# Joined count banks, shared sum and block banks, degrees through DRAM and fewer signals in a two-layer graph network kernel

## The chip, the cores and the metric

The kernel runs on one core of a Trainium2 chip. The metric is device time in microseconds; a lower number is better. Several runs are timed and one more is profiled. Engines are named as the profile names them: PE (matrix products), PEld (its weight loads), DVE (vector), ACT (scalar), POOL (GpSimd, which here issues the indirect gathers) and SP (which here issues most other DMAs).

## What is computed

A graph with 12,500 nodes of 256 features and 200,000 edges, sorted by their destination, goes through two layers that average over neighbours, a last product, and a residual with layer norm:

```python
def _sage_conv(x, src, dst, W_l, b_l, W_r):
    msgs = x[src]
    agg = jax.ops.segment_sum(msgs, dst, num_segments=N_NODES)
    deg = jax.ops.segment_sum(jnp.ones((src.shape[0],), x.dtype), dst, num_segments=N_NODES)
    mean = agg / jnp.maximum(deg, 1.0)[:, None]
    return mean @ W_l + b_l + x @ W_r
h = jax.nn.relu(_sage_conv(x, src, dst, W1_l, b1, W1_r))
h = jax.nn.relu(_sage_conv(h, src, dst, W2_l, b2, W2_r))
x = _layernorm(x + h @ W3 + b3, axis=-1)
```

Destinations are drawn as a squared uniform number, so low-numbered nodes have many edges and high-numbered ones few.

## The kernel before, in words

The edges lie in tiles of 128 (`NT` = 1563), the nodes in 98 blocks of 128. Two ways of summing neighbours run side by side in each layer.

**Gathered destinations.** Destinations beyond the first 1280 (layer 1) or 1792 (layer 2) are summed from gathered rows. A round (`Gathers.gathered`, L237) takes four edge tiles: POOL issues four indirect DMAs (L243), each fetching 128 rows of 256 floats into one of four `got` buffers. PE then multiplies each tile by a 0/1 selection of 32 columns (`one`, made by DVE at L201, two rounds ahead), so that four strips of 32 rows of one PSUM bank hold sums (L254; in layer 1 a 257th column of ones counts edges). A group has one or two rounds. At its end ACT copies the strips to SBUF (L259). `summed` (L262) multiplies them by a second selection `two` (L265) to place 128 sums, transposed, in PSUM; in layer 1 another product at L270 places the edge counts in one row. DVE adds both into a ring of 8 blocks (`degs` L273, `sums` L277). Layer 1 has 269 rounds and 186 groups, layer 2 has 247 rounds and 175 groups.

**Counted destinations.** The first destinations are done in seven groups of 256 with a matrix of edge counts. `count` (L646) builds it: for each edge tile DVE makes a selection of (destination, source block) pairs (`pick`, L661, three buffers, two tiles ahead) and of the source's low bits (L665); PE multiplies them (L706, L710 adds the edges that the next tile shares). A tile covers 5, 7 or 9 destinations of 98 source blocks each, 490, 686 or 882 columns. One PSUM bank holds 512, so 7 and 9 take two `halves`, each with a bank of `count_pool` (three banks) and a copy by ACT (L712, or an add by DVE at L697 for the first 128 tiles). `product` (L628) then multiplies the counts by all node rows, split into three bf16 parts: 98 steps of six matmuls (L638); SP loads `rows` for two steps at a time (L635, 384 KB, three buffers). `split_rows` (L622) makes the three parts of x for layer 1: SP loads a block, ACT and DVE take turns on it (L617 to L620), SP stores it (L626).

**Blocks.** When a block's sums are complete, `first_block` (L878, three pieces) or `last_block` (L902, five pieces) computes its output: load x or h, transpose it on PE (L839) and copy it on ACT (L842), multiply by both weights (`sage`, L863 and L865), add bias and scale by the reciprocal degree on DVE (L868, L869), apply relu on ACT (L871), store. For a ring block of layer 1, PE turns the row of degrees into a column with a matmul by one (L886), the same ACT copy brings it out, and DVE makes the reciprocal (L889, L890). ACT zeroes the used part of the ring (L894, L895, L913).

**Order.** PE and POOL keep the order in which the program is written (L421: `manual_schedule`); for DVE, ACT and SP a scheduler picks the order from estimated times, and each engine runs its own order strictly. `layer` (L562) writes the order: each round has three turns; in each, `pieces` advances one block piece (at most two blocks at a time, a block at most every second turn, `MOST, APART = 2, 2`), and `fill` adds steps of the counted work up to a cost that is due by then (`COST_DENSE`, `count_cost`). Stage 0 of layer 1 mixes counting with the 98 splits; later stages mix counting one group with the product of the one before.

**PSUM.** There are eight banks: one for strips (`part_ps`), one for `sum_ps`, two for blocks (`block_ps`), one for the product (`dense_ps`) and three for counts (`count_ps`):

```python
    sum_pool = ctx.enter_context(tc.tile_pool(name="sum_ps", bufs=1, space=PSUM))
    block_pool = ctx.enter_context(tc.tile_pool(name="block_ps", bufs=2, space=PSUM))
    dense_pool = ctx.enter_context(tc.tile_pool(name="dense_ps", bufs=1, space=PSUM))
    count_pool = ctx.enter_context(tc.tile_pool(name="count_ps", bufs=3, space=PSUM))
```

Of the kernel before, what the change touches and what calls it, by code (L numbers as in the profile page):

```python
# [7 lines left out]
F32 = mybir.dt.float32  # L8
# [11 lines left out]
POOL = mybir.EngineType.Pool  # L20

# [26 lines left out]
def by_runs(  # L48
# [80 lines left out]
    count_d = dram.tile([HG1 - 1, P, NB, DN], BF16, name="count_d")  # L129

# [43 lines left out]
    sum_pool = ctx.enter_context(tc.tile_pool(name="sum_ps", bufs=1, space=PSUM))  # L174
# [41 lines left out]
    class Gathers:  # L216
# [20 lines left out]
        def gathered(self, i):  # L237

            (gr, r), g = self.rounds[i], got[i % NGOT]
            t0, n = groups[gr]  # L240
            for j in range(G):
                e = t0 + j * n + r - C0 * P
                nc.gpsimd.indirect_dma_start(  # L243
                    out=g[:, j, :D], out_offset=None, in_=self.table,
                    in_offset=bass.IndirectOffsetOnAxis(ap=src_t[:, e:e + 1], axis=0))
            if i + AHEAD < len(self.rounds):
                self.chosen[i + AHEAD] = select(*self.rounds[i + AHEAD], self.second)
# [5 lines left out]
            for j in reversed(range(G)):  # L253
                nc.tensor.matmul(part_ps[j * W:(j + 1) * W, :width], lhsT=one[:, j],  # L254
                                 rhs=g[:, j, :width], start=r == 0, stop=r == n - 1)
# [6 lines left out]
        def summed(self, gr, some, two, done):  # L262
            sum_ps = sum_pool.tile([P, NC + 1, P], F32, name="sum_ps")
# [5 lines left out]
            if self.width > D:  # L269
                nc.tensor.matmul(sum_ps[0:1, NC], lhsT=some[:, D:D + 1], rhs=two,  # L270
# [284 lines left out]
    block_pool = ctx.enter_context(tc.tile_pool(name="block_ps", bufs=2, space=PSUM))  # L555
    dense_pool = ctx.enter_context(tc.tile_pool(name="dense_ps", bufs=1, space=PSUM))
    count_pool = ctx.enter_context(tc.tile_pool(name="count_ps", bufs=3, space=PSUM))
# [70 lines left out]
    def product(g, table3, c_sb):  # L628
# [3 lines left out]
        for b in range(NB):  # L632
            if b % 2 == 0:
                rows = work.tile([P, 2, 3, D], BF16, name="rows", bufs=3)
                nc.sync.dma_start(rows, table3[:, b:b + 2])  # L635
            for k in range(3):
                for c in range(NC):
                    nc.tensor.matmul(ps[:, c], lhsT=rows[:, b % 2, k, c * P:(c + 1) * P],  # L638
                                     rhs=c_sb[:, b, :DN],
                                     start=False, stop=b == NB - 1 and k == 2 and c == NC - 1)  # L640
            yield COST_DENSE
# [4 lines left out]
    def count(g, to):  # L646
# [32 lines left out]
        for t in range(lo_g, highs[g]):  # L679
# [5 lines left out]
            halves = [(0, w)] if w * NB <= 512 else [(0, w - w // 2), (w - w // 2, w)]  # L685
            if t < FIRST:
                j = t % G
                if j == 0:
                    pss = [count_pool.tile([P, 512], F32, name="count_ps") for _ in halves]
                for (a, b), ps in zip(halves, pss):  # L690
                    nc.tensor.matmul(ps[:, :(b - a) * NB], lhsT=s, rhs=r[:, a * NB:b * NB],
                                     start=j == 0, stop=j == G - 1)
                if j == G - 1:
                    n0 = off_dve.at(t - j)
                    for (a, b), ps in zip(halves, pss):
                        into = to[:, :, bass.ds(n0 + a, b - a)]
                        nc.vector.tensor_tensor(  # L697
                            into, into, ps[:, :(b - a) * NB].rearrange("p (d s) -> p s d", s=NB),
                            op=OP.add)
                yield count_cost(t)  # L700
            else:
                n0 = off_act.at(t)
                for a, b in halves:
                    ps = count_pool.tile([P, 512], F32, name="count_ps")
                    alone = a > 0 or before is None
                    nc.tensor.matmul(ps[:, :(b - a) * NB], lhsT=s, rhs=r[:, a * NB:b * NB],  # L706
                                     start=True, stop=alone)
                    if not alone:

                        nc.tensor.matmul(ps[:, :NB], lhsT=before[0], rhs=before[1],  # L710
                                         start=False, stop=True)
                    nc.scalar.copy(to[:, :, bass.ds(n0 + a, b - a)],  # L712
                                   ps[:, :(b - a) * NB].rearrange("p (d s) -> p s d", s=NB))
                    yield count_cost(t) / len(halves)
# [113 lines left out]
    def load_rows(table, n_rows, b, name):  # L828
        t = work.tile([P, D], F32, name=name)
# [6 lines left out]
    def transposed(t, ps, name, more=0):  # L836
# [481 lines left out]
```

## Time and profile before

| | |
|---|---|
| median of three runs | 2908.94 us (2904.64 to 2911.25) |
| profiled execution | 2910.6 us, span 2908.8 us |
| mean granted clock of PE | 0.914 |
| gathers of x (layer 1) | 1076, mean 1038 ns; the last ends at 1566 us |
| gathers of h (layer 2) | 988, mean 958 ns; from 1598 to 2856 us |
| products L638 | 7056, mean 279 ns, 976.9 us |
| count copies L712 on ACT | 1052 in three forms: 128x294 mean 650, 128x392 mean 663, 128x490 mean 721 ns |
| edge-count product L270 | 372 records (two to an fp32 matmul), 74.6 us |
| degree turn L886 | 176 records, 35.9 us |

In the profile an fp32 matmul shows as two records. Matmuls overlap, so the mean of a record is longer than the step from one start to the next. `L243 POOL ... x1076 | 1116.7, 1038 | 446.5 <-issue 274.2` reads: 1076 instructions, 1116.7 us busy, 1038 ns each, and the engine stood idle for 446.5 us before them, 274.2 of it with nothing in the profile to wait for.

### The profile page before, as it was taken

What the parts mean: (1) busy time and instruction counts of PE and PEld (TensorE: products, weight loads), DVE (VectorE), ACT (ScalarE), POOL (GpSimd) and SP (SyncE); (2) the same over time, 40 slices, a digit from 0 to 9 for tenths busy, and PEclk for the clock granted to TensorE, in tenths of its full rate; (3) what the DMA queues carried; (4) which work ended last, traced back from release to release, by engine and by line L of the source; (5) the groups of instructions that cost most, each with busy time, mean ns of one, the idle gap of its engine ahead of it and who ended that gap; (6) DMA issues with size and microseconds to landing.
All of it is one profiled execution on the core that took longest, in us unless ns stands there. A gap on an engine that the chain in (4) does not pass through costs nothing.

```text
span 2908.8 us, 54100 instructions
## 1 busy us (share of the span) xinstructions
PE 2394.6 (82%) x18630; PEld 1632.6 (56%) x18630; DVE 1471.2 (51%) x4350; ACT 1253.6 (43%) x2702; POOL 2065.3 (71%) x2074
## 2 busy tenths in 40 slices
PE   3475755898998999999996677877889898899995
PEld 1132323565665666666764455555666666677774
DVE  6687764664554565566564124434323333444443
ACT  0422764675675676677673014444112122222222
POOL 5777764777777777777774777777777777777772
PEclk9676767998999999999998899889999999999998
DMA  4455668877877878767864677777989989888872
GB/s 124 128 174 164 198 188 271 260 232 235 277 228 247 273 227 292 248 215 225 251 203 124 214 246 231 219 220 230 296 284 305 299 287 291 276 265 266 266 251 71
DMA packets 408133, 676.44 MB, mean 233 GB/s; under 512 B 59659, under 2 KB 266537, under 8 KB 407849
## 3 DMA queue, kind: packets, MB, share of 16 engines
q1 hardware_dynamic: 303415, 400.51, 42.5%
q0 software_dynamic: 99072, 270.66, 30.5%
q8 instruction: 149, 2.44, 0.3%
q10 hardware_dynamic: 5362, 1.72, 0.3%
q14 instruction: 135, 1.11, 0.1%
HBM read 582.80 MB, written 89.87 MB: 231 GB/s over the span
## 4 chain that ended last, share of the span: by engine, by line
PE 54%; DMA 19%; POOL 8%; issue 7%; DVE 6%; ACT 4%; DVEq 0%; SPq 0%; ACTq 0%; POOLq 0%
PE dense_ps L638 19%; POOL got L243 8%; PE part_ps L254 7%; PE block_ps L863 6%; DMA got<-h_d,src_t 5%; PE count_ps L706 5%; PE block_ps L865 5%; PE sum_ps L265 4%; DMA x_sb<-in_x_dram 3%; DMA rows<-h_d 3%; DMA rows<-x_d 3%; PE block_ps L839 2%; PE block_ps L921 2%; DMA split_sb<-in_x_dram 2%; PE sum_ps L270 2%
## 5 line engine op out<-in xcount | busy, mean ns | idle before, releaser
L243 POOL DMA_INDIRECT got<-in_x_dram,src_t x1076 | 1116.7, 1038 | 446.5 <-issue 274.2
L243 POOL DMA_INDIRECT got<-h_d,src_t x988 | 946.4, 958 | 343.1 <-issue 285.3
L638 PE MATMUL dense_ps<-counts,rows 128*128 128x256 bf16 x7056 | 976.9, 279 | 51.3 <-DMA rows<-h_d 27.7
L712 ACT CAST counts<-count_ps 128x392 f32 (+2 forms) x1052 | 717.6, 682 | 290.2 <-PE count_ps L710 174.0
L638 PEld LDWEIGHTS <-rows 128*128 128x128 bf16 x7056 | 671.3, 100 | 287.5 <-issue 88.6
L254 PE MATMUL part_ps<-got,one 128*32 128x257 f32 (+1 forms) x4128 | 359.7, 422 | 192.1 <-DMA got<-h_d,src_t 123.0
L706 PE MATMUL count_ps<-pick,low 128*128 128x392 bf16 (+2 forms) x1052 | 343.4, 354 | 57.0 <-ACT counts L712 27.0
L661 DVE TENSOR_SCALAR pick<-steps,key_t 128x686 bf16<-128x686 f16 (+2 forms) x748 | 301.4, 413 | 127.6 <-PE count_ps L706 110.2
L201 DVE TENSOR_TENSOR one<-lo_t,lane_b 128x128 f32<-128x128 bf16 x516 | 149.1, 289 | 372.7 <-PE part_ps L254 370.5
L259 ACT COPY some<-part_ps 128x257 f32<-128x257 f32 (+1 forms) x361 | 136.1, 377 | 431.4 <-PE part_ps L254 428.2
L254 PEld LDWEIGHTS part_ps<-got,one 128*32 128x32 f32 x4128 | 85.9, 111 | 323.5 <-issue 176.4
L265 PE MATMUL sum_ps<-two,some 128*128 128x128 f32 x1444 | 238.2, 290 | 0.2 <-DVE sums L277 0.2
L265 PEld LDWEIGHTS sum_ps<-two,some 128*128 128x128 f32 x1444 | 205.0, 201 | 20.5 <-issue 8.7
L277 DVE TENSOR_TENSOR sums<-sums,sum_ps 128x256 f32 x361 | 148.4, 411 | 132.6 <-PE sum_ps L265 101.9
L868 DVE TENSOR_TENSOR own<-block_ps,biases 128x256 f32<-128x256 f32 x196 | 83.0, 423 | 230.9 <-PE block_ps L865 230.2
L706 PEld LDWEIGHTS <-low 128*128 128x128 bf16 x1052 | 101.8, 100 | 152.3 <-DVE pick L661 54.2
L842 ACT COPY own_t<-block_ps 128x256 f32<-128x256 f32 (+1 forms) x294 | 110.0, 375 | 123.7 <-PE block_ps L839 121.2
L871 ACT ACTIVATE h<-own 128x256 f32<-128x256 f32 x196 | 81.4, 415 | 179.3 <-DVE own L869 179.2
L665 DVE TENSOR_TENSOR low<-low_t,lane_b 128x512 bf16<-128x512 bf16 x187 | 127.9, 684 | 21.1 <-PE count_ps L710 20.5
L710 PE MATMUL count_ps<-aft,low 128*128 128x98 bf16 x614 | 131.9, 215 | 0.0
L863 PE MATMUL block_ps<-w1l_sb,sums 128*128 128x256 f32 x352 | 113.9, 452 | 2.1 <-DVE sums L277 1.8
L863 PE MATMUL block_ps<-w2l_sb,sums 128*128 128x256 f32 x336 | 104.1, 437 | 11.3 <-DVE sums L277 11.1
(180 smaller groups left out, 2495.1 us busy)
## 6 DMA issues: line engine op xcount, KB each, us to landing
rows<-h_d SPq DMA_DIRECT2D x343, 384.0 KB
rows<-x_d SPq DMA_DIRECT2D x245, 384.0 KB
count_d<-counts SPq DMA_DIRECT2D x28, 896.0 KB
counts<-count_d SPq DMA_DIRECT2D x28, 896.0 KB
x_sb<-in_x_dram SPq DMA_DIRECT2D x194, 128.0 KB
x_d<-parts SPq DMA_DIRECT2D x98, 192.0 KB
h_d<-parts SPq DMA_DIRECT2D x98, 192.0 KB
got<-in_x_dram,src_t POOLq DMA_INDIRECT x1076
```

The costliest lines, as they stand in the source:

```text
L201: nc.vector.tensor_tensor(one, lo[:, a:a + n * (G - 1) + 1:n].unsqueeze(2).to_broadcast([P, G, W]), lane_b[:, :W].unsqueeze(1).to_broadcas ...
L243: nc.gpsimd.indirect_dma_start(out=g[:, j, :D], out_offset=None, in_=self.table, in_offset=bass.IndirectOffsetOnAxis(ap=src_t[:, e:e + 1], ...
L254: nc.tensor.matmul(part_ps[j * W:(j + 1) * W, :width], lhsT=one[:, j], rhs=g[:, j, :width], start=r == 0, stop=r == n - 1)
L259: nc.scalar.copy(some[:, :width], part_ps[:, :width])
L265: nc.tensor.matmul(sum_ps[:, c], lhsT=some[:, c * P:(c + 1) * P], rhs=two, start=True, stop=True)
L277: nc.vector.tensor_add(own, own, sum_ps[:, :NC])
L638: nc.tensor.matmul(ps[:, c], lhsT=rows[:, b % 2, k, c * P:(c + 1) * P], rhs=c_sb[:, b, :DN], start=False, stop=b == NB - 1 and k == 2 and ...
L661: nc.vector.tensor_scalar(r[:, :w * NB], steps[:, :w * NB], key_t[g][:, t - lo_g:t - lo_g + 1], None, op0=OP.is_equal)
L706: nc.tensor.matmul(ps[:, :(b - a) * NB], lhsT=s, rhs=r[:, a * NB:b * NB], start=True, stop=alone)
L712: nc.scalar.copy(to[:, :, bass.ds(n0 + a, b - a)], ps[:, :(b - a) * NB].rearrange("p (d s) -> p s d", s=NB))
L863: nc.tensor.matmul(ps[:, 0], lhsT=agg[:, c], rhs=wl[:, c], start=c == 0, stop=c == NC - 1)
L865: nc.tensor.matmul(ps[:, 1], lhsT=own_t[:, c], rhs=wr[:, c], start=c == 0, stop=c == NC - 1)
```

## The change

Six edits are made together.

- A counted tile takes one tile of two joined PSUM banks (`[P, 1024]`, laid so that the first five destinations end at the bank's border) and is copied or added once. There are two such tiles in layer 1 and one in layer 2, where there were three single banks.
- In layer 1 `sum_ps` and `block_ps` rotate through the same two banks (`mixed_pool`). In layer 2 sums keep these two, and blocks get two of their own.
- The edge counts are placed in bf16: the high halves of the fp32 words are used for both operands.
- The row of degrees goes to a DRAM tensor (`deg_d`) when the block begins, and comes back as a column at its next piece. L886 goes, and `overlap` and `ring` are called one piece earlier.
- Extra dependences make one instruction wait for all: the first strip matmul waits for all four gathers, the load of `rows` waits for the strip after the products that used the buffer (and has four buffers), the first product of `sage` waits for the ACT copy, and the zeroing of the ring waits for the last product. The built program's matmuls that signal fall from 5480 to 2612; the wait instructions on PE rise from 423 to 1452.
- `h_sb` shares buffers with `split_sb`, and `z` with `own`, which has two.

The core of the diff:

```diff
@@ -171,7 +174,11 @@
     part_pool = ctx.enter_context(tc.tile_pool(name="part_ps", bufs=1, space=PSUM))
-    sum_pool = ctx.enter_context(tc.tile_pool(name="sum_ps", bufs=1, space=PSUM))
+    mixed_pool = ctx.enter_context(tc.tile_pool(name="mixed_ps", bufs=2, space=PSUM))
+    strips, used = [], []
+    NROWS = 4
@@ -238,11 +245,13 @@
             t0, n = groups[gr]
+            landing = []
             for j in range(G):
                 e = t0 + j * n + r - C0 * P
-                nc.gpsimd.indirect_dma_start(
+                rows = nc.gpsimd.indirect_dma_start(
                     out=g[:, j, :D], out_offset=None, in_=self.table,
                     in_offset=bass.IndirectOffsetOnAxis(ap=src_t[:, e:e + 1], axis=0))
+                landing.append(rows.ins.name)
             if i + AHEAD < len(self.rounds):
@@ -251,8 +260,13 @@
             for j in reversed(range(G)):
-                nc.tensor.matmul(part_ps[j * W:(j + 1) * W, :width], lhsT=one[:, j],
-                                 rhs=g[:, j, :width], start=r == 0, stop=r == n - 1)
+                strip = nc.tensor.matmul(part_ps[j * W:(j + 1) * W, :width], lhsT=one[:, j],
+                                         rhs=g[:, j, :width], start=r == 0, stop=r == n - 1)
+                for name in landing:
+                    tc.add_manual_dep(strip.ins, name, LANDED, reason="rows of the other strips")
+                landing = []
+            strips.append(strip.ins.name)
             if r < n - 1:
@@ -260,14 +274,16 @@
         def summed(self, gr, some, two, done):
-            sum_ps = sum_pool.tile([P, NC + 1, P], F32, name="sum_ps")
+            sum_ps = mixed_pool.tile([P, 4, P], F32, name="sum_ps", tag="mixed")
             for c in range(NC):
...
             if self.width > D:
-                nc.tensor.matmul(sum_ps[0:1, NC], lhsT=some[:, D:D + 1], rhs=two,
+                nc.tensor.matmul(sum_ps[0:1, NC], lhsT=some[:, D:D + 1].bitcast(BF16)[:, 1:2],
+                                 rhs=two.bitcast(BF16).rearrange("p (n h) -> p n h", h=2)[:, :, 1],
                                  start=True, stop=True)
@@ -631,13 +645,18 @@
             if b % 2 == 0:
-                rows = work.tile([P, 2, 3, D], BF16, name="rows", bufs=3)
-                nc.sync.dma_start(rows, table3[:, b:b + 2])
+                rows = work.tile([P, 2, 3, D], BF16, name="rows", bufs=NROWS)
+                load = nc.sync.dma_start(rows, table3[:, b:b + 2])
+                if len(used) >= NROWS and used[-NROWS] < len(strips):
+                    tc.add_manual_dep(load.ins, strips[used[-NROWS]], LANDED, reason="products done")
             for k in range(3):
...
                                      start=False, stop=b == NB - 1 and k == 2 and c == NC - 1)
+            if b % 2:
+                used.append(len(strips))
             yield COST_DENSE
@@ -682,36 +701,33 @@
             w = room(t)
-            halves = [(0, w)] if w * NB <= 512 else [(0, w - w // 2), (w - w // 2, w)]
+            halves = [(a, min(a + 5, w)) for a in range(0, w, 5)]
             if t < FIRST:
...
                 if j == 0:
-                    pss = [count_pool.tile([P, 512], F32, name="count_ps") for _ in halves]
-                for (a, b), ps in zip(halves, pss):
-                    nc.tensor.matmul(ps[:, :(b - a) * NB], lhsT=s, rhs=r[:, a * NB:b * NB],
+                    ps = count_pool.tile([P, 1024], F32, name="count_ps")
+                    c = ps[:, 512 - 5 * NB:][:, :w * NB]
+                for a, b in halves:
+                    nc.tensor.matmul(c[:, a * NB:b * NB], lhsT=s, rhs=r[:, a * NB:b * NB],
                                      start=j == 0, stop=j == G - 1)
                 if j == G - 1:
-                    n0 = off_dve.at(t - j)
-                    for (a, b), ps in zip(halves, pss):
-                        into = to[:, :, bass.ds(n0 + a, b - a)]
-                        nc.vector.tensor_tensor(
-                            into, into, ps[:, :(b - a) * NB].rearrange("p (d s) -> p s d", s=NB),
-                            op=OP.add)
+                    into = to[:, :, bass.ds(off_dve.at(t - j), w)]
+                    nc.vector.tensor_tensor(into, into, c.rearrange("p (d s) -> p s d", s=NB), op=OP.add)
                 yield count_cost(t)
             else:
-                n0 = off_act.at(t)
+                ps = count_pool.tile([P, 1024], F32, name="count_ps")
+                c = ps[:, 512 - 5 * NB:][:, :w * NB]
                 for a, b in halves:
-                    ps = count_pool.tile([P, 512], F32, name="count_ps")
                     alone = a > 0 or before is None
-                    nc.tensor.matmul(ps[:, :(b - a) * NB], lhsT=s, rhs=r[:, a * NB:b * NB],
+                    nc.tensor.matmul(c[:, a * NB:b * NB], lhsT=s, rhs=r[:, a * NB:b * NB],
                                      start=True, stop=alone)
...
-                        nc.tensor.matmul(ps[:, :NB], lhsT=before[0], rhs=before[1],
+                        nc.tensor.matmul(c[:, :NB], lhsT=before[0], rhs=before[1],
                                          start=False, stop=True)
-                    nc.scalar.copy(to[:, :, bass.ds(n0 + a, b - a)],
-                                   ps[:, :(b - a) * NB].rearrange("p (d s) -> p s d", s=NB))
-                    yield count_cost(t) / len(halves)
+                nc.scalar.copy(to[:, :, bass.ds(off_act.at(t), w)], c.rearrange("p (d s) -> p s d", s=NB))
+                yield count_cost(t)
             before = s, aft
@@ -856,42 +871,58 @@
-    def sage(own_t, b, agg, wl, wr, bias, name):
-        ps = block_pool.tile([P, 2, D], F32, name="block_ps")
+    def sage(own_t, copied, b, agg, of_ring, wl, wr, bias, name):
+        ps = block_bank()
         for c in range(NC):
-            nc.tensor.matmul(ps[:, 0], lhsT=agg[:, c], rhs=wl[:, c], start=c == 0, stop=c == NC - 1)
+            product = nc.tensor.matmul(ps[:, 0], lhsT=agg[:, c], rhs=wl[:, c], start=c == 0,
+                                       stop=c == NC - 1)
+            if c == 0:
+                tc.add_manual_dep(product.ins, copied, LANDED, reason="the other products' rows")
         for c in range(NC):
-            nc.tensor.matmul(ps[:, 1], lhsT=own_t[:, c], rhs=wr[:, c], start=c == 0,
-                             stop=c == NC - 1)
-        own = work.tile([P, D], F32, name="own", bufs=1)
+            product = nc.tensor.matmul(ps[:, 1], lhsT=own_t[:, c], rhs=wr[:, c], start=c == 0,
+                                       stop=c == NC - 1)
+        if of_ring:
+            zeroed = nc.scalar.copy(agg, zeros)
+            tc.add_manual_dep(zeroed.ins, product.ins.name, LANDED, reason="it signals for all")
+        own = work.tile([P, D], F32, name="own")
         nc.vector.tensor_add(own, ps[:, 1], bias)
...
+    def block_bank():
+        if block_pool is None:
+            t = mixed_pool.tile([P, 4, P], F32, name="block_ps", tag="mixed")
+        else:
+            t = block_pool.tile([P, 4, P], F32, name="block_ps")
+        return t.rearrange("p (two a) l -> p two (a l)", two=2)
     def turned():
-        t = block_pool.tile([P, 2, D], F32, name="block_ps")
+        t = block_bank()
         return t.rearrange("p two (a l) -> p (two a) l", l=P)
...
         of_ring = agg is None
-        yield True
-        ps = turned()
         if of_ring:
...
             agg, deg_row = ring(b)
-            nc.tensor.matmul(ps[:, NC, 0:1], lhsT=deg_row, rhs=ones[0:1, 0:1], start=True, stop=True)
-        x_t, deg = transposed(x_sb, ps, "own_t", int(of_ring))
+            nc.sync.dma_start(deg_d[b:b + 1], deg_row)
+        yield True
+        if of_ring:
+            deg = work.tile([P, 1], F32, name="deg")
+            with nc.allow_non_contiguous_dma(reason="a row becomes a column"):
+                nc.sync.dma_start(deg, deg_d[b, :, None])
+        x_t, copied = transposed(x_sb, turned(), "own_t")
+        yield True
         if of_ring:
...
             nc.vector.reciprocal(rdeg[:, b:b + 1], deg)
-        yield True
-        h, own = sage(x_t, b, agg, w1l_sb, w1r_sb, biases[:, 0], "h")
+        h, own = sage(x_t, copied, b, agg, of_ring, w1l_sb, w1r_sb, biases[:, 0], "h")
         if of_ring:
-            nc.scalar.copy(agg, zeros)
             nc.scalar.copy(deg_row, zeros[0:1, 0])
@@ -900,26 +931,24 @@
     def last_block(b, agg=None):
-        h_sb = load_rows(h_d, NB * P, b, "h_sb")
+        h_sb = load_rows(h_d, NB * P, b, "h_sb", "split_sb")
         of_ring = agg is None
...
             agg, _ = ring(b)
-        h_t, _ = transposed(h_sb, turned(), "own_t")
+        h_t, copied = transposed(h_sb, turned(), "own_t")
         yield True
-        h2, _ = sage(h_t, b, agg, w2l_sb, w2r_sb, biases[:, 1], "h")
-        if of_ring:
-            nc.scalar.copy(agg, zeros)
+        h2, _ = sage(h_t, copied, b, agg, of_ring, w2l_sb, w2r_sb, biases[:, 1], "h")
         x_sb = load_rows(x, N, b, "x_sb")
...
         yield True
-        y = block_pool.tile([P, 2, D], F32, name="block_ps")
+        y = block_bank()
         for c in range(NC):
             nc.tensor.matmul(y[:, 0], lhsT=h2_t[:, c], rhs=w3_sb[:, c], start=c == 0, stop=c == NC - 1)
-        z = work.tile([P, D], F32, name="z")
+        z = work.tile([P, D], F32, name="z", tag="own")
         nc.vector.tensor_add(z, y[:, 0], x_sb)
@@ -934,12 +963,16 @@
-    layer(gathers_1, first_block, 3, staged(stages_1), cost_of(stages_1))
+    block_pool = None
+    with tc.tile_pool(name="count_ps", bufs=2, space=PSUM) as count_pool:
+        layer(gathers_1, first_block, 3, staged(stages_1), cost_of(stages_1))
+    block_pool = ctx.enter_context(tc.tile_pool(name="block_ps", bufs=2, space=PSUM))
+    count_pool = ctx.enter_context(tc.tile_pool(name="count_ps", bufs=1, space=PSUM))
     layer(Gathers(h_d, True), last_block, 5, staged(stages_2), cost_of(stages_2))
     with tc.tile_pool(name="result", bufs=1) as su:
-        bad_ps = block_pool.tile([P, 2, D], F32, name="block_ps")
+        bad_ps = block_bank()
         nc.tensor.matmul(bad_ps[0:1, 0, :TESTS], lhsT=ones, rhs=bad, start=True, stop=True)
...
         nc.vector.tensor_reduce(n_bad, bad_ps[0:1, 0, :TESTS], axis=mybir.AxisListType.X, op=OP.add)
```

More of the change, by code (lines that the diff above doesn't have):

```diff
@@ L20 @@
 POOL = mybir.EngineType.Pool
+LANDED = mybir.DependencyInfo(mybir.DependencyClass.Sync, mybir.DependencyReason.DATA)
 P = 128
@@ L129, in by_runs @@
     count_d = dram.tile([HG1 - 1, P, NB, DN], BF16, name="count_d")
+    deg_d = dram.tile([NB, P], F32, name="deg_d")
     src_t = consts.tile([P, (CH - C0) * P], I32, name="src_t")
@@ L554, in by_runs @@
     work = ctx.enter_context(tc.tile_pool(name="work", bufs=2))
-    block_pool = ctx.enter_context(tc.tile_pool(name="block_ps", bufs=2, space=PSUM))
     dense_pool = ctx.enter_context(tc.tile_pool(name="dense_ps", bufs=1, space=PSUM))
-    count_pool = ctx.enter_context(tc.tile_pool(name="count_ps", bufs=3, space=PSUM))
     MOST, APART = 2, 2
@@ L825, in cost_of, with load_rows @@
         return whole
-    def load_rows(table, n_rows, b, name):
-        t = work.tile([P, D], F32, name=name)
+    def load_rows(table, n_rows, b, name, tag=None):
+        t = work.tile([P, D], F32, name=name, tag=tag or name)
         n = min(P, n_rows - b * P)
@@ L834, in load_rows, with transposed @@
         return t
-    def transposed(t, ps, name, more=0):
+    def transposed(t, ps, name):
         for c in range(NC):
             nc.tensor.transpose(ps[:, c], t[:, c * P:(c + 1) * P], ident)
-        s = work.tile([P, NC * P + 1], F32, name=name)
-        n = NC * P + more
-        nc.scalar.copy(s[:, :n], ps.rearrange("p c l -> p (c l)")[:, :n])
-        return s[:, :NC * P].rearrange("p (c l) -> p c l", l=P), s[:, NC * P:]
+        s = work.tile([P, NC, P], F32, name=name)
+        copied = nc.scalar.copy(s, ps[:, :NC])
+        return s, copied.ins.name
     def ring(b):
```

## The prediction

> **What bounds the kernel now.** I read the page's first two parts, then the busy times by stretch, because the shares average stages with different limits.
>
> ```profile
> span 2908.8 us, 54100 instructions
> PE 2394.6 (82%) x18630; PEld 1632.6 (56%) x18630; DVE 1471.2 (51%) x4350; ACT 1253.6 (43%) x2702; POOL 2065.3 (71%) x2074
> ...
> POOL 5777764777777777777774777777777777777772
> ```
>
> PE looks like the bound, but POOL's digit hardly moves: 7 is its full rate. The timeline shows why.
>
> ```profile
> 1599.24 0.95 POOL L243 DMA_INDIRECT got<-h_d,src_t  x1 [0.31 <-issue]
> ```
>
> Each gather is followed by about 0.305 us in which POOL waits for nothing. So a stretch's POOL stall is its length, less busy time, less 0.305 us per gather. The table by stretch (length, then PE, PEld, DVE, ACT and POOL with counts, clock, DMA):
>
> ```profile
> 100.00:500.00 400.00, 248.16 (x1347) 115.93 (x1345) 287.42 (x796) 193.97 (x401) 274.55 (x256) 0.72 0.64 196
> 500.00:1000.00 500.00, 445.57 (x3795) 304.91 (x3796) 271.83 (x789) 323.06 (x656) 362.25 (x359) 0.94 0.78 249
> 1000.00:1500.00 500.00, 487.74 (x4161) 338.51 (x4159) 297.13 (x886) 344.17 (x709) 368.65 (x364) 0.99 0.77 244
> 1500.00:1598.00 98.00, 72.72 (x586) 50.48 (x583) 55.59 (x175) 51.54 (x125) 51.12 (x51) 0.91 0.42 126
> 1598.00:2100.00 502.00, 394.80 (x3036) 272.08 (x3037) 171.19 (x490) 154.52 (x311) 381.25 (x397) 0.92 0.75 234
> 2100.00:2856.00 756.00, 681.64 (x5423) 513.59 (x5422) 305.63 (x933) 166.97 (x465) 565.14 (x592) 0.97 0.86 276
> ```
>
> Row by row the stall is 47, 28, 20, 31, 0 and 10 us. The 31 is the turn between the layers, where gathers of h wait for its last store. After the last gather 53 us remain. So layer 2 has almost nothing to give, layer 1 about 95 us. With all 105 us of stall outside the turn gone the span would be about 2804: POOL's floor. Who causes the stalls differs: from 1000 to 1500 PE is 98% busy and causes them itself; in 370 to 550 the waits say (waiter, releaser: us, times, longest):
>
> ```profile
> POOL got L243 <- PE part_ps L254: 53.7, 11, 17.9
> ```
> ```profile
> PE block_ps L886 <- DVE own L869: 51.8, 6, 19.1
> ```
>
> and in 330 to 510, on DVE,
>
> ```profile
> DVE split_sb L618 <- ACT parts L617: 47.5, 34, 5.9
> ```
>
> There the row splitting holds DVE, DVE holds the PSUM banks, and PE does not free the gather buffers. Faster PE work does not help there.
>
> **PE work removed.** The PE timeline has start, duration of a merged group, group:
>
> ```profile
> 1003.07 0.61 PE L265 MATMUL sum_ps<-two,some 128*128 128x128 f32 x4
> 1003.61 0.38 PE L270 MATMUL sum_ps<-two,some 128*1 128x128 f32 x2
> 1003.93 0.30 PE L706 MATMUL count_ps<-pick,low 128*128 128x294 bf16 x1
> ```
> ```profile
> 1411.06 0.49 PE L638 MATMUL dense_ps<-counts,rows 128*128 128x256 bf16 x3
> 1411.48 0.38 PE L886 MATMUL block_ps<-ones,degs 1*128 1x1 f32 x2
> 1411.79 0.44 PE L839 MATMUL block_ps<-ident,x_sb 128*128 128x128 f32 x2
> ```
>
> Four L265 records step by 0.11 us, so the next could start at 1003.52; L706 starts at 1003.93. A degree row costs 0.41 us: two fp32 passes of 0.108 and about 0.19 of gaps where the tile's shape changes. In bf16 one pass stays: 98 bf16 columns (L710) step by 0.04 us, so 128 take 0.05; with both gaps 0.24. Saved: 0.17 x 186 = 32 us. L886 goes: three L638 of 0.109 end the step at 1411.39, L839 starts at 1411.79, so 0.40 x 88 = 35 us. Together 67 us, all in layer 1. By the counts per stretch (L270: 60, 90, 178 records, L886: 25, 56, 76, two to a matmul) it is 10 us in 100 to 500, 19 in 500 to 1000, 30 in 1000 to 1500, the rest around the turn.
>
> What of it counts: in 1000 to 1500 at most POOL's 20;[...] I take 15. In 500 to 1000 some 15 of the 28 belong to the split lag (505, 545 us); of the other 13 and part of the lag I take 14, with help from the fourth rows buffer, since PE waited 16 us for rows there. The early 10 us hide under the splits.
>
> **Signals.** The built program has 5480 matmuls that signal, after the change 2612. By the Trainium skill ("TensorE: Matmul & The Clock Gate", The cost: per-tile semaphore tail) every increment adds 26.3 ns at the end of a packed group, which would make 2868 x 0.026 = 75 us of PE time. The trace speaks otherwise:
>
> ```profile
> 1406.40 0.82 PE L638 MATMUL dense_ps<-counts,rows 128*128 128x256 bf16 x6
> 1407.05 0.37 PE L706 MATMUL count_ps<-pick,low 128*128 128x490 bf16 x1
> ...
> 1407.30 0.82 PE L638 MATMUL dense_ps<-counts,rows 128*128 128x256 bf16 x6
> 1407.96 0.61 PE L265 MATMUL sum_ps<-two,some 128*128 128x128 f32 x4
> ```
>
> The first six end with a signal, the second do not (by the trace's operands); the next start is 0.65 and 0.66 us later. A signal costs the issue nothing, so I take 0, not 75; the four signals of a strip group could still delay ACT a little. PE's wait instructions rise from 423 to 1452, 1053 of them before strips. Groups with such an instruction inside step as fast (0.109 us) when it is satisfied: 0 again, up to 0.05 x 1053 = 53 us if each were exposed.
>
> **Joined count banks.** 432 of 1052 copies go (tiles 7 and 9 wide). A pair now takes 650 + 663 or 721 + 663 ns (the three L712 forms); a fixed part of about 0.2 us falls away, 90 us of ACT in all. ACT is 43% busy and off the path; PE waited 27 us for count banks in all. Two double banks replace three single ones in layer 1: deeper for wide tiles, shallower for width 5. In layer 2 one double bank serves 64 tiles within some 250 us, 4 us each, against 0.5 of matmul and 1.2 of copy: covered, and POOL has no stall there. I take -2 for ACT's relief, between -10 and +10.
>
> **Shared banks, buffers, release by strips.** In layer 1 sums and blocks rotate through two banks: 89 + 2 x 42 uses in 1000 to 1500, one per 2.9 us, so a bank must be free 5.8 us later on average and 1.8 (one third of a round) when crowded; the DVE add that frees a sum takes 0.28 + 0.40. I take +3, bounds 0 and +15. In the split stage this makes PE no freer: DVE is late there. The rows loads have four buffers instead of three but wait for the next strip, up to a round of 5.4 us later: about even, a gain inside the 14 above. Queued behind that wait on SP are x_sb loads, stores and degrees. The second sum bank in layer 2 and later rows there touch 10 us of stall: -5.
>
> **Degrees through DRAM.** This is the added wait. Per ring block SP issues a 512-byte store (waits for DVE's degree add) and a read of 128 single elements (waits until the store lands); behind them on SP stand rows, splits and h stores; DVE's max and reciprocal wait for the read, with picks and selections behind. No such row exists; nearest is
>
> ```profile
> 1595.27 1.69 DMA h_d<-h
> ```
>
> from the chain: a 128 KB store lands in 1.69 us, two such make 3.4. The Trainium skill ("DMA: Bandwidth & Descriptors", Anatomy of one DMA) speaks against the change: about 2.0 us fixed plus bytes at 436 GB/s, fitted for DMAs that GpSimd issues. By it the row's store would take 2.3 and the trip 4.0; with some 18 blocks uncovered (13 in the split stage, 5 at the turn) the rule costs 0.6 x 18 = 11 us more than the row. I use the row. From begin to the block's product lie four turns of a third of a round (4 x 1.34 us a round), 7.2 us, so the trip is covered in the dense stages unless loaded queues (rows took 5 to 9 us there) stretch it. Not covered: the split stage, where SP is part of the loop. In SP's new order most pairs stand between two split loads and the stores that wait for their arithmetic, so most of the trip hides. Also the new order puts 49 splits instead of 45 before the 24th sum, into time where POOL is full anyway; the 98 splits run from 117 to 538 us, 4.3 each, so up to -17. Bounds -17 and +29 (13 x 2.2: the 3.4 less 1.2 that other waits on SP hide); I take -5. The 176 further issues of 0.32 us each on SP (the length of its other issues) fall into time in which SP waits: 0. At the turn some eight blocks run back to back: +4 for a trip that the last ones do not hide, bounds 0 and +15. DVE waiting for late degrees in the dense stages: 75 blocks x 0.05 = +4, bounds 0 and +15. Tail: z and own share two buffers, so z waits for an output store: +1.
>
> **Sum.** PE work -15 -14, copies -2, banks +3, layer 2 -5, tail +1: -32. Degrees -5 +4 +4: +3. Together -29. Span 2908.8 - 29 = 2880. The profiled execution took 2910.6, 1.8 around the span, and the median is 2908.94, 1.7 lower: 2880 for the median.
>
> **Rivals.** (A) The forecast, 0.42: 2862 to 2900. (B) More goes: deeper rows buffers and earlier splits clear the early stalls too, 2/3 of 105 us: 2838, reaching to 2810 if signals were as dear as the rule says, floor 2804; 0.25. For it: nearly all layer 1 stall is PE order. Against: splits and their DMAs stay. (C) The PE relief is real but POOL keeps its pace and losses cancel: 2906; 0.11. (D) Slower: the degree trip stops SP. Unhidden it costs its bounds, 29 in the split loop, 15 at the turn and 15 in the dense stages: 59 - 32 = +27, 2936. It decides once its uncovered part passes 32 us, 0.36 us for each of 88 blocks; against it stands SP's order; 0.22. The edit that fails to do what it says is the signal thinning, priced at 0 already.
>
> **Numbers.** About 0.2%, 6 us, is what a measurement can tell from no change. Faster: A and B, 0.67; same: C, 0.11; slower: D, 0.22. The range reaches halfway into B and D: 2832 to 2930; A alone has 2862 to 2900.
>
> **What would show it.** PE busy down about 70 us, no L886 row, the degree row at one record per sum near 0.24 us; POOL's mean unchanged and its stall in 1000 to 1500 below 10 us; strips still 0.64 us per group of eight records. Wrong: long waits of DVE's max on the degree read, SP waiting on the degree store over 2 us per block, or POOL's waits before 550 us above 54.

## The result and the profile after

| | before | after |
|---|---|---|
| median in the same set of runs | 2906.79 us | 2868.46 us (2859.28 to 2886.7) |
| profiled execution | 2910.6 us, span 2908.8 us | 2859.28 us, span 2857.5 us |
| last gather of layer 1 ends | 1566.1 us | 1532.8 us |
| gap to the first gather of h | 31.9 us | 24.0 us |
| first to last gather of h | 1257.6 us | 1247.7 us |
| after the last gather | 53.2 us | 52.9 us |

The ratio is 0.9876, 95% interval 0.9847 to 0.9905: 38 us of the median, against the 29 forecast. The profiled execution of after is the shortest of its four runs, so its own 51 us (33 in layer 1, 8 in the gap, 10 in layer 2) show where time went, not how much in the median.

The first two parts of the page after:

```profile
span 2857.5 us, 53445 instructions
PE 2325.8 (81%) x18268; PEld 1607.4 (56%) x18268; DVE 1461.6 (51%) x4334; ACT 1099.4 (38%) x2270; POOL 2054.2 (72%) x2074
...
POOL 5777775677777777777675777777777777777771
```

PE lost 68.8 us of busy time, ACT 154. In the table by stretch of after (columns as before) POOL does more gathers in each stretch:

```profile
100.00:500.00 400.00, 253.66 (x1452) 122.26 (x1451) 294.02 (x816) 202.96 (x430) 284.03 (x269) 0.75 0.69 208
500.00:1000.00 500.00, 434.13 (x3742) 304.35 (x3741) 271.92 (x788) 265.12 (x487) 366.27 (x366) 0.91 0.79 252
1000.00:1500.00 500.00, 465.68 (x4148) 333.95 (x4140) 305.61 (x928) 292.90 (x548) 374.17 (x368) 0.98 0.77 240
```

By the same sum as in the prediction (length, less busy, less 0.305 us per gather) POOL's stall is 33.9, 22.1 and 13.6 us, where it was 47.4, 28.3 and 20.3. The PE timeline of after has the degree row as one bf16 record:

```profile
1002.85 0.61 PE L279 MATMUL sum_ps<-two,some 128*128 128x128 f32 x4
1003.39 0.22 PE L285 MATMUL sum_ps<-two,some 128*1 128x128 bf16 x1
1003.54 0.38 PE L723 MATMUL count_ps<-pick,low 128*128 128x490 bf16 x1
```

Four steps of 0.108 end at 1003.28, the count starts at 1003.54: the row costs 0.26 us (0.41 before, 0.24 forecast). PE's waits after (waiter, releaser: us, times, longest) hold one that is new and two that grew (in before, L638 waited for the same loads):

```profile
PE dense_ps L655 <- DMA rows<-h_d: 41.1, 20, 5.6
PE sum_ps L279 <- DVE own L890: 38.6, 4, 23.5
...
PE dense_ps L655 <- DMA rows<-x_d: 33.9, 19, 4.8
```

Before:

```profile
PE dense_ps L638 <- DMA rows<-h_d: 27.7, 18, 3.9
...
PE dense_ps L638 <- DMA rows<-x_d: 23.4, 15, 3.3
```

The new one, L279, is the old split lag in a new place: the sum's bank is now one that a late block holds.

### The profile page after: what moved, and what is told of

It is laid out like the page before. It is cut to its first block, busy times and chain, and to the rows that moved or that the text cites. A ratio compares the mean times of both kernels' runs of the same rounds, so it can differ in the third digit from the quotient of the medians.

```text
span 2857.5 us, 53445 instructions
## 1 busy us (share of the span) xinstructions
PE 2325.8 (81%) x18268; PEld 1607.4 (56%) x18268; DVE 1461.6 (51%) x4334; ACT 1099.4 (38%) x2270; POOL 2054.2 (72%) x2074
## 4 chain that ended last, share of the span: by engine, by line
PE 45%; DMA 24%; POOL 11%; issue 8%; DVE 7%; ACT 4%; SPq 1%; DVEq 0%; ACTq 0%; POOLq 0%
PE dense_ps L655 17%; POOL got L251 11%; PE part_ps L263 6%; PE block_ps L878 5%; DMA got<-h_d,src_t 4%; DMA rows<-h_d 4%; PE block_ps L883 4%; PE count_ps L723 4%; DMA x_sb<-in_x_dram 4%; PE sum_ps L279 4%; DMA rows<-x_d 4%; DMA split_sb<-in_x_dram 3%; DMA got<-in_x_dram,src_t 2%; PE block_ps L950 2%; PE block_ps L855 2%
## 5 line engine op out<-in xcount | busy, mean ns | idle before, releaser
L655 PE MATMUL dense_ps<-counts,rows 128*128 128x256 bf16 x7056 | 958.4, 279 | 75.4 <-DMA rows<-h_d 41.1
L729 ACT CAST counts<-count_ps 128x686 f32 (+2 forms) x620 | 540.2, 872 | 237.8 <-PE count_ps L723 188.0
L723 PE MATMUL count_ps<-pick,low 128*128 128x490 bf16 (+2 forms) x1052 | 321.1, 359 | 62.5 <-ACT counts L729 37.2
L273 ACT COPY some<-part_ps 128x257 f32<-128x257 f32 (+1 forms) x361 | 134.5, 373 | 414.2 <-PE part_ps L263 413.1
L279 PE MATMUL sum_ps<-two,some 128*128 128x128 f32 x1444 | 240.9, 293 | 39.4 <-DVE own L890 38.6
L279 PEld LDWEIGHTS sum_ps<-two,some 128*128 128x128 f32 x1444 | 209.4, 205 | 55.3 <-DVE own L890 39.9
L886 ACT COPY sums<-zero 128x256 f32<-128x256 f32 x172 | 69.3, 403 | 393.4 <-PE block_ps L883 391.8
L723 PEld LDWEIGHTS <-low 128*128 128x128 bf16 x1052 | 105.0, 101 | 140.0 <-DVE pick L680 33.6
L857 ACT COPY own_t<-block_ps 128x256 f32<-128x256 f32 x294 | 108.8, 372 | 125.6 <-PE block_ps L855 124.5
```

The lines of the kernel that those rows point to most:

```text
L273: nc.scalar.copy(some[:, :width], part_ps[:, :width])
L279: nc.tensor.matmul(sum_ps[:, c], lhsT=some[:, c * P:(c + 1) * P], rhs=two, start=True, stop=True)
L723: nc.tensor.matmul(c[:, a * NB:b * NB], lhsT=s, rhs=r[:, a * NB:b * NB], start=True, stop=alone)
L729: nc.scalar.copy(to[:, :, bass.ds(off_act.at(t), w)], c.rearrange("p (d s) -> p s d", s=NB))
```

## The experiments

Theory 1 is the prediction's: the 67 us of PE work that leave layer 1 make the gain. Theory 2: the thinned signals do (26 ns of PE time for each, by the rule that the prediction cites). Theory 3: ACT's relief and the deeper buffers do. Each kernel was timed on the same chip as the kernel before, in one set of runs; ratios are to that. One part undone is compared with after's 0.9876 from another set, and where intervals overlap this is said. The stall is POOL's, summed by stretch in the profile of each.

| kernel | ratio, 95% interval | stall 100 to 500, to 1000, to 1500 us |
|---|---|---|
| before | 1 | 47, 28, 20 |
| after | 0.9876 (0.9847 to 0.9905) | 34, 22, 14 |
| before + degree edits | 0.9888 (0.9873 to 0.9904) | 34, 20, 9 |
| after - degree edits | 0.9949 (0.9929 to 0.9970) | 50, 23, 30 |
| after, fp32 degree row | 0.9917 (0.9887 to 0.9946) | 35, 16, 27 |
| after, degrees turned on PE | 0.9926 (0.9901 to 0.9950) | 43, 26, 13 |
| after, two copies | 0.9886 (0.9860 to 0.9912) | 35, 26, 14 |
| after, banks apart | 0.9920 (0.9893 to 0.9947) | 40, 17, 13 |
| after, no extra dependences | 0.9830 (0.9813 to 0.9846) | 31, 13, 7 |
| after, rows released by products | 0.9837 (0.9810 to 0.9865) | 43, 8, 4 |
| the same, 3 rows buffers, deeper splits | 0.9816 (0.9783 to 0.9850) | 12, 6, 12 |

**Before with the degree edits alone.** L270 in bf16, and L886 replaced by the store and read of `deg_d`, as in the diff above; nothing else.

> The kernel before with only the two degree edits: the bf16 degree row and the degrees' trip through DRAM. Theory 1 (the prediction's): the gain is the 67 us of PE work that leaves layer 1; this kernel alone gets most of it, -29 +3 = -26, so about 2882 (2872 to 2893), with the last gather of layer 1 some 20 to 30 us earlier. Theory 2 (fewer signals give the gain): within 6 us of the kernel before. Theory 3 (ACT's relief by single copies and the deeper rows buffers give it): within 6 us of the kernel before.

2872.84 us against 2905.41: 33 us, and 33 of the 96 us of stall. Theories 2 and 3 would have left this kernel where it was; theory 1 holds, with 7 us more than forecast. This kernel cannot be told from after (0.9888 and 0.9876): the other edits together add nothing measurable to the degree edits.

**After without the degree edits.** The same two edits taken out of after.

> The changed kernel with only the two degree edits undone (fp32 degree row, degrees turned by a matmul on PE). Theory 1: most of the gain is lost, 2868 + 26 = 2894 (2884 to 2906). Theories 2 and 3: it keeps the gain, 2868 to 2875.

2890.11 us: 21 of after's 36 us are lost at 2905, and the stall in 1000 to 1500 is 30 us. In layer 1 the rest of the change gains nothing (its last gather ends at 1562 us); what it keeps, 15 us, lies in the gap (23.5 us) and in layer 2. So the rest is worth 15 us without the degree edits and about 3 with them; the values of the parts do not add up.

**After without the four extra dependences.** 

```diff
-                for name in landing:
-                    tc.add_manual_dep(strip.ins, name, LANDED, reason="rows of the other strips")
...
-                if len(used) >= NROWS and used[-NROWS] < len(strips):
-                    tc.add_manual_dep(load.ins, strips[used[-NROWS]], LANDED, reason="products done")
...
-            if c == 0:
-                tc.add_manual_dep(product.ins, copied, LANDED, reason="the other products' rows")
...
-            tc.add_manual_dep(zeroed.ins, product.ins.name, LANDED, reason="it signals for all")
```

> The changed kernel without the four extra dependences: 5012 matmuls signal instead of 2612, PE has 613 wait instructions instead of 1452, and the rows load waits for its own products again. Theory 1: signals and satisfied waits cost nothing, 2868 within 6. Theory 2 (26 ns of PE time for each of 2400 signals, 63 us of PE, shielded as the degrees' 67 us are): 2868 + 27 = 2895. If the wait instructions cost their 51 ns records, this one is faster by up to 20: 2848.

2859.65 us, 0.0046 below after: 2400 more signals and the kernel is faster. Theory 2 falls, though not by this run alone, since it also releases rows earlier (the next run parts the two). On PE's timeline of this kernel six products, the last of them with a signal, still step to the next start in 0.65 us:

```profile
1408.32 0.82 PE L650 MATMUL dense_ps<-counts,rows 128*128 128x256 bf16 x6
1408.97 0.37 PE L718 MATMUL count_ps<-pick,low 128*128 128x490 bf16 x1
```

**After with rows released by their products.** Only the second dependence of the diff above is taken out.

> The changed kernel with only the extra dependence of the rows load undone: a load waits for the products that used its buffer, not for the next strip; the strips' and blocks' dependences stay (PE keeps 1464 wait instructions, 3140 matmuls signal). Theory R (the late release of rows made PE wait 75 us for rows, against 18 or less without the dependences): all of the 9 us that the run without the four dependences gained come back, 2860 within 6. Theory W (PE's wait instructions before strips cost the 9 us): no gain, 2868 within 5.

2850.1 us against 2900.61, 0.0039 below after; the intervals overlap, but the groups of the page show the cause. After:

```profile
L655 PE MATMUL dense_ps<-counts,rows 128*128 128x256 bf16 x7056 | 958.4, 279 | 75.4 <-DMA rows<-h_d 41.1
```

This kernel:

```profile
L653 PE MATMUL dense_ps<-counts,rows 128*128 128x256 bf16 x7056 | 950.5, 278 | 5.1 <-DMA rows<-x_d 4.9
```

Theory R holds for the wait; the time is clear of after's interval only in the run without all four. The strips' and blocks' dependences, which this kernel keeps, show neither cost nor gain beside the kernel without any: 3140 signals and 1464 wait instructions on PE against 5012 and 613, at 0.9837 and 0.9830. So theory W falls too.

**After with the degree row in fp32.** L285 written as L270 was.

> The changed kernel with only the degree row back in fp32: 186 x 0.17 = 32 us of PE work added to layer 1 and nothing else. If PE work in layer 1 counts as the prediction took it (29 of 67, 0.43 of its time): +14, 2882. If it counts as in the run of before with the degree edits alone (33 of 67): +16. If the gain lay in the trip through DRAM (its earlier reciprocal): within 4 of 2868.

2876.32 us, 0.0041 or 12 us above after (intervals overlap): of 32 us of PE work 12 reach the time, a share of 0.37. In 1000 to 1500 13 us of stall come back; over the three stretches it is 8.

**After with degrees turned on PE.** The trip's two DMAs out, the matmul of L886 back.

> The changed kernel with only the degrees' trip undone: PE turns the row with a matmul again, 88 x 0.40 = 35 us of PE work added, no DMA of degrees. At 0.43 to 0.5 of PE time +15 to +17, less what the trip costs, which I took as 3: +12, 2880. If the trip costs nothing: 2884. If it costs as much as it saves: 2868.

2880.03 us, 0.0050 or 15 us above after (intervals just overlap). At 0.37 the 35 us of PE work would cost 13, so the trip itself costs about 13 - 15 = -2 us. Each of the two differences is uncertain by 11 us or more (from the intervals), so this says only that the trip costs little.

**After with two copies per joined tile.**

```diff
-                nc.scalar.copy(to[:, :, bass.ds(off_act.at(t), w)], c.rearrange("p (d s) -> p s d", s=NB))
+                n0 = off_act.at(t)
+                for a, b in halves:
+                    nc.scalar.copy(to[:, :, bass.ds(n0 + a, b - a)],
+                                   c[:, a * NB:b * NB].rearrange("p (d s) -> p s d", s=NB))
```

> The changed kernel with its joined banks, but each 7 or 9 wide tile copied in two halves of 5 and the rest: 432 copies more, some 170 us of ACT work. Theory 1: ACT is far from full, +2, at most +10: 2868 to 2878. Theory 3 (ACT's relief is a main part of the gain): +20 or more, 2888 to 2900, and PE's wait for count banks grows by as much.

2872.62 us, 0.0010 above after: 3 us, no difference that this measures. ACT's busy time rises by 146 us (1099.4 to 1245.5), PE's wait for count banks from 37 to 56. Theory 3 falls for ACT.

**After with the banks apart.** 

```diff
-    mixed_pool = ctx.enter_context(tc.tile_pool(name="mixed_ps", bufs=2, space=PSUM))
+    mixed_pool = ctx.enter_context(tc.tile_pool(name="mixed_ps", bufs=1, space=PSUM))
...
-    block_pool = None
-    with tc.tile_pool(name="count_ps", bufs=2, space=PSUM) as count_pool:
+    with (tc.tile_pool(name="count_ps", bufs=2, space=PSUM) as count_pool,
+          tc.tile_pool(name="block1_ps", bufs=1, space=PSUM) as block_pool):
```

> The changed kernel with the two shared banks of layer 1 given out apart, one to sums and one to blocks (layer 2: one bank for sums again, two for blocks). Theory 1 (sharing costs 3, the sums' new wait of 39 us for a block's bank being mostly where POOL is stalled anyway): 2862 to 2868. Rival (two banks for blocks are what the turn between the layers and the dense stages need; alone, turn and product of two blocks follow each other in one bank): +10 or more, 2878 up, and the gap between the layers grows from 24 us to 32 or more.

2875.71 us, 0.0044 or 13 us above after (intervals overlap), so sharing more likely gains than costs. Layer 2 has a single bank for sums again here, but is as long as in after (1248.7 and 1247.7 us). The rival's place is not confirmed: the gap is 25.7 us, and the stall sum 69.9 as after's 69.6. PE waits for a block's bank (L855 for L890, 41 us, 13 times) instead of a sum's. In its profile gathers are longer by 13 us in all (POOL busy 2067.6 to 2054.2); what makes them so stays open.

**Three rows buffers; three and deeper splits; `own` doubled in before.** In this set of runs every kernel, the kernel before too, took 17% longer (before: 3414.45 us), so only its ratios are used. The first kernel has `NROWS = 3` and no dependence of the rows load; the second adds the first diff to it; the third is before with the second diff.

```diff
-        s = work.tile([P, 3, D], BF16, name="parts")
+        s = work.tile([P, 3, D], BF16, name="parts", bufs=3)
-        t = work.tile([P, D], F32, name=name, tag=tag or name)
+        t = work.tile([P, D], F32, name=name, tag=tag or name,
+                      bufs=3 if "split_sb" in (name, tag) else 2)
```

```diff
-        own = work.tile([P, D], F32, name="own", bufs=1)
+        own = work.tile([P, D], F32, name="own")
...
-        z = work.tile([P, D], F32, name="z")
+        z = work.tile([P, D], F32, name="z", tag="own")
```

> The changed kernel with rows released by their products (no extra dependence of the load) and three buffers as before instead of four. Theory R (what costs is the late release, and the fourth buffer only made up for part of it): 0.984 to 0.987 of the kernel before, as with four buffers released by products (0.984). Rival (the fourth buffer is what helps, the release is harmless): PE's wait for rows comes back, 0.988 or more.

0.9892 (0.9865 to 0.9919).

> The run with three rows buffers released by products, and the freed memory given to the row splitting: three buffers for its input and three for its parts instead of two. In the written order 50 instead of 31 splits then stand before DVE's 24th sum. If the POOL stall around 460 to 530 us (16 + 5 + 11 + 9 us in the run without the rows dependence) is the splits' lag behind PE's order, as the prediction read it: half or more of it goes, 20 us, 0.977 to 0.980 of before, and PE no longer waits about 20 us at once for a block's add on DVE. If that stall comes from DMA traffic or from ACT's copies: no change, 0.984 to 0.987.

0.9831 (0.9801 to 0.9861).

> The kernel before with one edit of the change: own has two buffers instead of one, shared with z. If own's single buffer is what makes the last blocks of layer 1 follow each other slowly: the gap between the layers goes from 32 to about 24 us, and the time to 0.997 of before. If the gap's 8 us come from the count banks, the rows or ACT's relief: the gap stays at 31 or more, and the time within 0.001.

0.9921 (0.9894 to 0.9948), with a gap of 34.8 us. Three rows buffers gave the rival's number, but waits are longer here, so this alone does not decide for other chips. The deeper splits gain 0.006 (the intervals part: 0.9861 and 0.9865). In the traces 66 splits, not 50, stand before DVE's 24th sum in that kernel, and 49 in after.

The second `own` gains 0.008 here where 0.003 was expected; why is open. Its gap cannot be set beside the 31.9 us of before: the kernel with deeper splits has a gap of 33.6 us in this set and 24.8 in the next. What it did at the turn is taken up below.

**The deeper splits again.**

> The same kernel as the run with three rows buffers released by products and three buffers for the row splitting, since in that call the kernel before itself took 3414 us instead of about 2905. If the splits' lag makes the POOL stall of 460 to 530 us: where the kernel before takes about 2905, 0.976 to 0.981 of it, about 2840, and POOL's stall from 100 to 1000 us is 20 to 30 us instead of the 52 of the run without the rows dependence. If not: 0.984 or more, the stall unchanged.

2851.75 us against 2904.11. The table by stretch of this kernel has, from 100 to 500,

```profile
100.00:500.00 400.00, 274.41 (x1569) 132.48 (x1569) 309.15 (x870) 219.81 (x465) 302.58 (x279) 0.75 0.73 224
```

a stall of 12.3 us, 19 with the next stretch, where the kernel with rows released by products had 51. In 440 to 535 after had, among PE's waits,

```profile
PE sum_ps L279 <- DVE own L890: 36.1, 3, 23.5
```

and this kernel has no such wait. So the splits' lag makes that stall (the kernel compared also has four rows buffers instead of three; nothing links those to this wait). Of the 33 us of stall removed there little reaches the time: with three rows buffers PE waits 67 us for rows again, gathers from 100 to 500 take 1085 instead of 1047 ns (11 us), and layer 2 is 7 us longer. It lies 0.0060 below after (the intervals just overlap), and cannot be told from the kernel with rows released by products.

## Why the prediction held, point by point

**The sum, -29 against -36 to -38: right in its main term, and helped by luck.** The degree edits, forecast at -26, carry it. Among the rest, misses cancelled: the late release of rows, taken as about even, cost some 11 us, and the turn gained 8 where it was to lose 4.

**PE work, -29: right, from a sum that had the places wrong.** The edits alone in before gave -33, taken out of after +21, one by one +12 and +15. The forecast put 15 in 1000 to 1500, 14 in 500 to 1000 and nothing but the splits' -5 before; in before with these edits alone the stall in these three fell by 11, 8 and 13. The early third comes with the degree edits, not with the rest: without them after's stall in 100 to 500 is 50. It goes with the turn's edit (stall 43 with that undone, 35 with the fp32 row back), one profile each. That does not show that faster PE work helped there: the fp32 row alone, 5 us of PE work in this stretch, moved nothing, and undoing the turn also moves the degrees' waits on DVE. Nor was it the earlier splits alone: 49 stand before DVE's 24th sum in after, as forecast, but 46 in before with the degree edits, where before had 45. Which part of the turn's edit did it stays open.

**Signals, 0 against the Trainium skill's 75: right.** The rule ("TensorE: Matmul & The Clock Gate", The cost: per-tile semaphore tail) is about packed groups; taken for every signal, it would have made the kernel with 2400 more signals 63 us of PE time dearer. It is 13 us faster at 2905, for which the earlier release of rows accounts. Beside the kernel with rows released by products, 1872 signals fewer, the rule asks for 49 us; the times are the same, and PE's busy time is 2329.8 against 2316.1 us, at granted clocks of 0.916 and 0.927.

**Copies, -2: right, with twice the relief that was forecast.** ACT's copies fell from 717.6 to 540.2 us, 177, not 90. In the groups by form of after:

```profile
L729 ACT CAST counts<-count_ps 128x882 f32 x212 | 214.5, 1012 | 93.3 <-PE count_ps L723 87.9 <-ACT sums L886 0.7 <-PE sum_ps L285 0.6
L729 ACT CAST counts<-count_ps 128x686 f32 x220 | 189.9, 865 | 107.8 <-PE count_ps L723 100.1 <-DVE aft L690 1.9 <-ACT degs L926 0.8
L729 ACT CAST counts<-count_ps 128x490 f32 x188 | 135.7, 722 | 36.6 <-PE count_ps L727 26.9 <-DVE most L735 5.7 <-ACT parts L633 0.7
```

From 490 to 882 columns a copy grows by 0.74 ns per column, which leaves a fixed 0.36 us, not 0.2 (a figure that the three forms named in the prediction do not give); the run with two copies paid 146 us for 432, 0.34 each. (Narrower copies do not lie on this line: 294 columns took 650 ns in before.) ACT is off the path, so twice the relief changed the time no more.

**Rows, about even: right, but I took both halves as small.** With three buffers released by products PE waits 73 us for rows (before with the degree edits), with four and the late release 75, with four released by products 5. By these waits the fourth buffer brings nothing until the late release is gone. Taking that out gained some 11 us (0.0039; 0.0046 with the other three dependences out too).

**Shared banks, +3: probably wrong in sign.** Undone, the time grows by 13 (intervals overlap), with the stall unchanged, so how sharing would gain is not shown. The bank wait that I priced came (39 us), but stood in for the wait that a block's bank had caused before (52 us).

**The turn, +4: wrong by 12.** I looked at the trip, and not at the order and at `own`. With the degree edits alone the gap did grow by 4.2 us, to 36.1 (one profile each); the other edits took 12 off. In before the last two counted blocks (weights times `d_sb`) run at the very end, 11 us before the first gather of h:

```profile
1586.86 1.13 PE L863 MATMUL block_ps<-w1l_sb,d_sb 128*128 128x256 f32 x4 [0.46 <-ACT own_t L842]
1588.69 1.03 PE L863 MATMUL block_ps<-w1l_sb,d_sb 128*128 128x256 f32 x4
```

After, they are done 43 to 47 us before it:

```profile
1509.87 1.23 PE L878 MATMUL block_ps<-w1l_sb,d_sb 128*128 128x256 f32 x4
1514.15 1.13 PE L878 MATMUL block_ps<-w1l_sb,d_sb 128*128 128x256 f32 x4
```

The second cause is `own`. In before each late block takes 3.3 us or more, since DVE starts the next only when the single `own` is free, right behind L620:

```profile
1590.03 0.43 DVE L620 TENSOR_TENSOR parts<-own,parts 128x256 bf16<-128x256 f32 x1 [0.47 <-ACT parts L619]
1590.56 0.42 DVE L868 TENSOR_TENSOR own<-block_ps,biases 128x256 f32<-128x256 f32 x1
...
1593.32 0.42 DVE L620 TENSOR_TENSOR parts<-own,parts 128x256 bf16<-128x256 f32 x1 [0.47 <-ACT parts L619]
1593.85 0.42 DVE L868 TENSOR_TENSOR own<-block_ps,biases 128x256 f32<-128x256 f32 x1
```

In before with a second `own`, which keeps the late place, they follow faster:

```profile
1798.03 0.42 DVE L868 TENSOR_TENSOR own<-block_ps,biases 128x256 f32<-128x256 f32 x1
...
1799.49 0.42 DVE L868 TENSOR_TENSOR own<-block_ps,biases 128x256 f32<-128x256 f32 x1 [0.32 <-PE block_ps L865]
```

From the end of the last product of a block to the first gather of h 7.4 us pass in before and 7.8 with the degree edits alone, but 4.3 with a second `own` (in the slower set) and 4.3 in after (4.2 to 5.1 in all kernels built on it). So some 3 of the 8 us are the second `own`'s. The other 5 lie before that product's end, where the two blocks' products, 3.7 us, are gone. All traced kernels built on after have the early place, and before and the two kernels built on it have the late one, so it comes with the other edits, most likely the one yield per joined tile in the written order. That was not tried alone.

**The trip, +3 in all with its order: right within the error.** Between the store's issue and DVE's max lie 3.4 us at the least, as estimated from the h store's row, and 6.5 in the median, within the 7.2 us that the prediction counted from a block's begin to its product. DVE's max waited for the read, but on an engine that is half idle:

```profile
DVE deg L922 <- DMA deg<-deg_d: 69.2, 46, 4.1
```

Rival D's mechanism is there (SP waits 36 us for the stores) at a price too small for these runs to show.

**Layer 2, -5, and tail, +1:** layer 2 is 10 us shorter, the tail 0.3. But before with the degree edits alone, whose layer 2 has no edit, is 7 us shorter there too, so single profiles can't confirm the 5.

The claim that POOL's stall in 1000 to 1500 falls below 10 failed for after (13.6); with rows released by products it is 4.

## What to carry to other kernels

Where an engine that is not the busiest on the page paces a stage, count its stall by stretch: of 67 us of PE work removed, 21 to 33 reached the time, and the stall table showed 33 both ways. An edit that replaces many releases by one late one can spend the buffer that it came with: look at the waits of what is released, not at the number of signals. And at stage ends compare the written order and the buffers too: two blocks that moved away from a turn and a second buffer outweighed the cost that was being estimated there.

## What was not expected of the hardware

One set of runs was on a chip where the same program took 3414 instead of about 2905 us at a granted clock of 0.87 instead of 0.92. The gathers took as long as ever; the idle time before them grew, and so did PE's busy time. The kernel with three rows buffers and deeper splits there:

```profile
L251 POOL DMA_INDIRECT got<-in_x_dram,src_t x1076 | 1112.6, 1034 | 631.5 <-issue 268.3
```

The same kernel on the other chip had 382.7 us of idle time there at 1044 ns, and its PE was busy for 2334.9 us instead of 2530.4. In the kernel with three rows buffers ACT waited 295.4 us (69 times) at L273 with the releaser given only as remote. The cause of the slower set is open.
